# Attention as numerators times a value-output product Y, from seven products of quarters, in an order written by hand

## The chip, the cores and the metric

The kernel runs on one core of a Trainium2 chip. The metric is device time of one launch in microseconds (us), as the median of several runs. A core has five engines that run side by side, each with its own queue of instructions in a fixed order: TensorE (PE) multiplies matrices into PSUM, VectorE (DVE) and ScalarE (ACT) do elementwise work, GpSimd (POOL) does slower elementwise work and can issue transfers, SyncE (SP) issues transfers. An instruction that waits holds everything behind it on its own engine. All data are f32; every f32 product on PE is two instructions with one weight load (PEld) each, called passes here.

## The reference

One transformer block with adaptive layer norm, four batches of 1024 tokens of width 512. Cut to what matters:

```python
mod = (_silu(c) @ wmod).reshape(4, 6, 1, -1)          # sa, ca, ga, sb, cb, gb
ga = (2 * (ga >= 0) - 1) * jnp.maximum(jnp.abs(ga), 0.25)   # gb alike
h = _layernorm(x) * (1 + ca) + sa
qf, kf = h @ Wq.T, h @ Wk.T                            # rank 64, shared by all 16 heads
attn = softmax(qf @ kf.T)                              # 1024 x 1024, the same for each head
x = x + ga * ((attn @ (h @ Wv.T)) @ Wo.T)
h = _layernorm(x) * (1 + cb) + sb
x = x + gb * ((h @ factors.sum(0)) / sqrt(8) + bias)   # eight factors of 512 x 512
```

The scores carry a factor for each head that is one, so all heads have the same probabilities. Wv and Wo can therefore be multiplied into one 512 x 512 matrix, and the softmax's division can be left until the end: the kernels keep numerators (exponents) and scale by the inverse of their sum where the result is added onto x.

## The kernel before

Tokens lie in eight tiles of 128 rows for each batch, x in 16 buffers (two batches). The weights' product `wvo` is made once (line 152). For each batch:

- LN1 (`ln1`): statistics on DVE, the inverse square root as a power on POOL (`rstd_of`, line 276), normalized tokens `xn_a` by DVE (line 290). They are turned into channels-first form `hT_a`: for batch 0 by PE, for the others by a DVE transpose of 32 x 32 blocks and 16 small transfers for each half (`hT_by_dma`, `move_blocks`, line 340), the first half issued by SP, the second by ACT.
- Projection to queries and keys (`project`, line 385), with the scale 1 + ca put into the weights and the shift sa as a bias.
- Scores, exponents, transposition (`scores`, lines 428 to 449; `transpose_probs`, line 455) in four pairs of row tiles: PE, a maximum on DVE, exponents on ACT, a block transpose on DVE, and 16 transfers on SP for each pair.
- Z, the numerators times the normalized tokens, channels first (`z_steps`, line 492, two halves of 512 tokens), copied by ACT; then `attn_out` (line 533): Z times `w` (wvo scaled by 1 + ca and ga), divided and added onto x by DVE (line 538). The constant part that comes from sa is added with `add_c1` (line 332).
- LN2 (`ln2`), its transposition with 16 transfers on ACT for each half (line 569; for the last batch by PE), the scale and shift on ACT (line 572), and the bias added onto x by DVE (line 577).
- `ffn` (line 592): the hidden tile times `f`, the sum of the eight factors scaled by gb; added onto x by DVE (line 597), stored, and x of the batch after next loaded into the buffer.

The sum of the factors (`sum_factors`, lines 259 to 265) is made once, on POOL: 32 loads of 128 x 512 into three buffers, and 28 adds, while batch 0 is in its first Z products. The eight products of F of one batch stand among the Z products of the next. The order in which instructions of each engine stand was set by a scheduler that ranks the steps of the loop at line 630.

Of the kernel before, what the change touches and what calls it, by code (L numbers as in the profile page):

```python
# [10 lines left out]
F32 = mybir.dt.float32  # L11
# [5 lines left out]
def weave(main, fill):  # L17

    done = 0
    for k, step in enumerate(main):  # L20
        step()
        want = (k + 1) * len(fill) // len(main)
        while done < want:
            fill[done]()
            done += 1
    for step in fill[done:]:
        step()
# [3 lines left out]
def kernel(  # L31
# [23 lines left out]
    NT = T // P  # L55
    GT = NT // 2
    GW = GT * P
    Q = 32
# [6 lines left out]
    xnp = ctx.enter_context(tc.tile_pool(name="xnp", bufs=1))  # L65
    stg = ctx.enter_context(tc.tile_pool(name="stg", bufs=3))
    hp = ctx.enter_context(tc.tile_pool(name="hp", bufs=2))
    qkp = ctx.enter_context(tc.tile_pool(name="qkp", bufs=1))
    prp = ctx.enter_context(tc.tile_pool(name="prp", bufs=2))
    stp = ctx.enter_context(tc.tile_pool(name="stp", bufs=1))  # L70
    ptp = ctx.enter_context(tc.tile_pool(name="ptp", bufs=2))
    ztp = ctx.enter_context(tc.tile_pool(name="ztp", bufs=2))
    wbp = ctx.enter_context(tc.tile_pool(name="wbp", bufs=1))
    bcp = ctx.enter_context(tc.tile_pool(name="bcp", bufs=1))
    small = ctx.enter_context(tc.tile_pool(name="small", bufs=4))
    dram = ctx.enter_context(tc.tile_pool(name="dram", bufs=1, space=bass.MemoryType.DRAM))
    ps_s = ctx.enter_context(tc.tile_pool(name="ps_s", bufs=2, space=PSUM))
    ps_m = ctx.enter_context(tc.tile_pool(name="ps_m", bufs=4, space=PSUM))

    def psum_mm(name):  # L80
        return ps_m.tile([P, 512], F32, tag="mm", name=name)


    ident = const.tile([P, P], F32, name="ident")
    make_identity(nc, ident)
    mhalf = const.tile([P, NT], F32, name="mhalf")
    nc.vector.memset(mhalf, -0.5)

# [6 lines left out]
    def load_x(b, t):  # L95
        tl = xp.tile([P, D], F32, tag="x", name=f"x_{b}_{t}")
        nc.sync.dma_start(out=tl, in_=x[b, ts(t, P), :])
        xt[b, t] = tl

    def xn_tile(name):
        return xnp.tile([P, GT, D], F32, tag="xn", bufs=4, name=name)

    wvs, wos = xn_tile("wvs"), xn_tile("wos")
    for cc in range(KC):
        nc.sync.dma_start(out=wvs[:, cc, :], in_=wv[ts(cc, P), :])
        nc.sync.dma_start(out=wos[:, cc, :], in_=woT[ts(cc, P), :])
        for t in range(2 * cc, 2 * cc + 2):
            load_x(0, t)  # L110


    wm_a = ptp.tile([P, 2, KC, D], F32, tag="pt", name="wm_a")
    wm_b = ptp.tile([P, 2, KC, D], F32, tag="pt", name="wm_b")
    wm_c = ztp.tile([P, KC, D], F32, tag="zt", name="wm_c")
    wm_d = ztp.tile([P, KC, D], F32, tag="zt", name="wm_d")
    wmods = [wm_a[:, 0], wm_a[:, 1], wm_b[:, 0], wm_b[:, 1], wm_c, wm_d]

    def load_wmod(m):
        nc.sync.dma_start(  # L120
            out=wmods[m], in_=wmod[:, ts(m, D)].rearrange("(kc p) e -> p kc e", p=P)
        )

    load_wmod(0)
    load_wmod(1)
    wqk = const.tile([P, KC, 2 * R], F32, name="wqk")
    nc.sync.dma_start(out=wqk, in_=wqkT.rearrange("(kc p) r -> p kc r", p=P))
    for m in range(2, 6):
        load_wmod(m)

    rows_a = wbp.tile([B, 4, D], F32, tag="w_b", name="rows_a")
    rows_b = wbp.tile([B, 4, D], F32, tag="f_b", name="rows_b")
    biasb = rows_a[:, 3, :]
    nc.sync.dma_start(out=biasb, in_=bias.to_broadcast([B, D]))
    for t in range(NT):
        load_x(1, t)

# [8 lines left out]

    wvo = const.tile([P, KC, D], F32, name="wvo")
    pw = [ps_s.tile([P, T], F32, tag="sc", name=f"ps_wvo_{h}") for h in range(2)]
# [10 lines left out]


    def mod_products(ms, name):
        ps = psum_mm(f"ps_mod_{name}")
        for kc in range(KC):
            for g, m in enumerate(ms):
                nc.tensor.matmul(
                    ps[32 * g : 32 * g + B, :], scT[:, kc, :], wmods[m][:, kc, :],
                    start=(kc == 0), stop=(kc == KC - 1),
                )
        return ps

    def mod_rows(ps, count, dst):
        rows = []
        for g in range(count):
            nc.vector.tensor_copy(dst[:, g, :], ps[32 * g : 32 * g + B, :])
            rows.append(dst[:, g, :])
        return rows

    def channels(rows, name, plus):

        ps = psum_mm(f"ps_ch_{name}")  # L180
        for kc in range(KC):
            nc.tensor.transpose(ps[:, ts(kc, B)], rows[:, ts(kc, P)], ident[0:B, 0:B])
        m = const.tile([P, KC, B], F32, name=f"mod_{name}")
        nc.vector.tensor_scalar(
            m.rearrange("p k b -> p (k b)"), ps[:, : KC * B], plus, None, ALU.add
        )
        return m

    def gate(g, name):

        sg = bcp.tile([B, D], F32, tag="bc_ga", name=f"gsign_{name}")
        ab = bcp.tile([B, D], F32, tag="bc_c", name=f"gabs_{name}")
# [4 lines left out]


    rows_d = {}

    def publish(rows, name):
        d = dram.tile([B, D], F32, name=f"rows_{name}")
        nc.sync.dma_start(out=d, in_=rows)
        rows_d[name] = d

    def spread(name, b):
        tag = f"bc_{name}" if name in ("ga", "gb") else "bc_c"
# [510 lines left out]
```

## Time and profile before

| | |
|---|---|
| median of three runs | 599.99 us (599.4 to 600.7) |
| span of the profiled execution | 596.5 us; the median is 3.5 us above it |
| PE busy | 565.6 us, 95% of the span |
| DVE, ACT, POOL busy | 311.5, 96.8 and 79.8 us |
| largest groups on PE | Z (L492) 225.3 us, F (L592) 112.2, Z times w (L533) 111.9 |
| scores, projections (L428, L385) | 45.9 and 35.2 us |
| transfers | 65.64 MB, 144703 packets |

The profile is of one execution. A page gives busy time of each engine, the span in 40 slices (a digit is a tenth of the slice), a chain of waits that ended last, and the costliest groups: line, engine, operation, output and inputs by the program's names, shapes, count, busy time, mean length in ns, and the idle time before them with its releaser. Passes on PE overlap, so their mean length is not their spacing; spacing is read from a timeline, as (length of a row less its last pass) divided by the count less one.

### The profile page before, as it was taken

The numbers are of one execution on the slowest core, as the hardware profiler recorded it, in microseconds if no ns is written. First come the engines' busy times: TensorE is split into PE (matmuls) and PEld (weight loads), VectorE is DVE, ScalarE is ACT, GpSimd is POOL, SyncE is SP. The second block draws the span as 40 slices with busy tenths as digits, with TensorE's granted clock in tenths as the row PEclk, the third lists the DMA queues.
The fourth block names the chain that finished last, engine by engine and source line by source line (L and its number), as shares of the span: only waits on it lengthen the run. The fifth ranks groups of instructions, "written<-read, shape, count | busy, mean of one in ns | idle before, by whom it ended". The sixth has DMA issues, their size and how long they took to land.

```text
span 596.5 us, 4491 instructions
## 1 busy us (share of the span) xinstructions
PE 565.6 (95%) x1424; PEld 242.9 (41%) x1424; DVE 311.5 (52%) x514; ACT 96.8 (16%) x161; POOL 79.8 (13%) x90
## 2 busy tenths in 40 slices
PE   6988999999999999799999999899999999999997
PEld 2434443334443344234444443333444434444443
DVE  4559903972695186054697168226398333015641
ACT  1224310241012200123012010022104020000010
POOL 1001017788700001000000001000000000000000
PEclk9998899999999999899999999879999999999999
DMA  8941356869267635204237735303316811000011
GB/s 306 381 177 35 85 114 182 215 167 223 86 109 146 193 105 143 70 4 95 49 58 152 207 113 158 83 1 71 71 23 124 187 59 68 0 0 0 2 70 70
DMA packets 144703, 65.64 MB, mean 110 GB/s; under 512 B 115732, under 2 KB 128532, under 8 KB 144680
## 3 DMA queue, kind: packets, MB, share of 16 engines
q1 hardware_dynamic: 84200, 46.47, 27.9%
q10 hardware_dynamic: 57600, 9.45, 8.8%
q0 software_dynamic: 2880, 9.44, 5.7%
q8 instruction: 11, 0.18, 0.1%
q14 instruction: 12, 0.10, 0.1%
HBM read 29.64 MB, written 8.42 MB: 64 GB/s over the span
## 4 chain that ended last, share of the span: by engine, by line
PE 75%; DVE 9%; DMA 4%; SPq 3%; ACTq 3%; issue 2%; ACT 1%; POOL 1%; POOLq 0%; DVEq 0%
PE ps_z L492 28%; PE ps_o L533 18%; PE ps_f L592 15%; PE ps_sc L428 6%; PE ps_qk L385 3%; ACTq L340 3%; PE ps_wvo L152 3%; SPq L340 2%; DVE st_a L353 2%; DVE x L332 2%; DMA hT_a<-st_a 1%; DVE xn_a L290 1%; DMA out_dram<-x 1%; DVE nm L443 1%; DVE w L515 1%
## 5 line engine op out<-in xcount | busy, mean ns | idle before, releaser
L492 PE MATMUL ps_z<-pt,xn_a 128*128 128x512 f32 x512 | 225.3, 595 | 0.0
L492 PEld LDWEIGHTS ps_z<-pt,xn_a 128*128 128x128 f32 x512 | 96.1, 190 | 126.6 <-issue 125.3
L592 PE MATMUL ps_f<-f,hT_f 128*128 128x512 f32 x256 | 112.2, 594 | 5.6 <-ACT hT_f L572 4.2
L533 PE MATMUL ps_o<-w,zt 128*128 128x512 f32 x256 | 111.9, 593 | 0.0
L592 PEld LDWEIGHTS ps_f<-f,hT_f 128*128 128x128 f32 x256 | 47.9, 190 | 65.6 <-issue 54.6
L533 PEld LDWEIGHTS ps_o<-w,zt 128*128 128x128 f32 x256 | 48.1, 190 | 60.4 <-issue 60.0
L538 DVE SCALAR_TENSOR_TENSOR x<-ps_o,ri,x 128x512 f32<-128x512 f32 x32 | 23.5, 743 | 79.7 <-PE ps_o L533 79.7
L597 DVE TENSOR_TENSOR x<-ps_f,x 128x512 f32<-128x512 f32 x32 | 22.0, 687 | 77.1 <-PE ps_f L592 77.1
L446 ACT ACTIVATE pr<-ps_sc,nm 128x1024 f32<-128x1024 f32 x32 | 35.6, 1114 | 123.0 <-DMA hT_f<-xn_f 58.2
L428 PE MATMUL ps_sc<-kT,qT 64*128 64x512 f32 x128 | 45.9, 691 | 8.6 <-DMA hT_a<-st_a 3.8
L502 ACT COPY zt<-ps_z 128x512 f32<-128x512 f32 x32 | 18.7, 585 | 214.1 <-PE ps_z L492 205.0
L276 POOL TENSOR_TENSOR r_f<-v_f,mhalf 128x4 f32<-128x4 f32 x8 | 9.3, 1158 | 286.6 <-DVE v_f L272 286.6
L443 DVE TENSOR_REDUCE nm<-ps_sc 128x1 f32<-128x1024 f32 x32 | 37.5, 1206 | 7.3 <-PE ps_sc L428 7.2
L385 PE MATMUL ps_qk<-hT_a,wqk 128*128 128x512 f32 x64 | 35.2, 704 | 2.8 <-DMA hT_a<-st_a 1.9
L455 DVE STREAM_TRANSPOSE pr<-pr 128x2048 f32<-128x2048 f32 x14 | 32.2, 2299 | 0.4
L264 POOL TENSOR_TENSOR fsum<-fsum,factor 128x512 f32<-128x512 f32 x24 | 30.9, 1288 | 1.6 <-DMA factor<-in_factors_dram 1.1
L428 PEld LDWEIGHTS ps_sc<-kT,qT 64*128 64x128 f32 x128 | 14.2, 203 | 36.5 <-ACT kT L403 12.6
L399 DVE TENSOR_SCALAR qT<-ps_qk,qbias 64x512 f32<-64x512 f32 x8 | 5.9, 742 | 43.4 <-PE ps_qk L385 43.4
L276 POOL TENSOR_TENSOR r_a<-v_a,mhalf 128x4 f32<-128x4 f32 x8 | 8.5, 1068 | 123.4 <-DVE v_a L272 123.4
L281 DVE BATCH_NORM_STATS2 bn_a<-x 128x6 f32<-128x512 f32 x32 | 21.0, 672 | 7.5 <-DMA x<-in_x_dram 7.4
L332 DVE TENSOR_TENSOR x<-x,bc_c 128x512 f32<-128x512 f32 x32 | 23.7, 792 | 1.4 <-DMA bc_c<-rows_c 1.4
L385 PEld LDWEIGHTS ps_qk<-hT_a,wqk 128*128 128x128 f32 x64 | 14.0, 227 | 24.2 <-issue 20.5
(87 smaller groups left out, 317.9 us busy)
## 6 DMA issues: line engine op xcount, KB each, us to landing
pt<-pr SPq DMA_DIRECT2D x224, 64.0 KB, 2.1
x<-in_x_dram SPq DMA_DIRECT2D x32, 256.0 KB, 4.0
factor<-in_factors_dram POOLq DMA_DIRECT2D x32, 256.0 KB, 3.4
out_dram<-x SPq DMA_DIRECT2D x32, 256.0 KB, 2.3
hT_f<-xn_f ACTq DMA_DIRECT2D x96, 64.0 KB, 2.1
hT_a<-st_a SPq DMA_DIRECT2D x48, 64.0 KB, 2.3
hT_a<-st_a ACTq DMA_DIRECT2D x48, 64.0 KB, 2.1
wm_a<-in_wmod_dram SPq DMA_DIRECT2D x2, 1024.0 KB
```

The source lines that it names most:

```text
L264: nc.gpsimd.tensor_tensor(fsum[:, kc, :], acc, f, ALU.add)
L332: nc.vector.tensor_tensor(xt[b, t], xt[b, t], bc, ALU.add)
L340: queue.dma_start(out=dst[ts(c, Q), :, ts(r, width)], in_=src[ts(r, Q), :, c])
L385: nc.tensor.matmul(ps[: 2 * R, :], wqkb[b][:, kc, :], hT[:, kc, :], start=(kc == 0), stop=(kc == KC - 1),)
L428: nc.tensor.matmul(ps[:, ts(h, 512)], qT[h * R : (h + 1) * R, ts(i, P)], kT[h * R : (h + 1) * R, :], start=True, stop=True,)
L443: nc.vector.tensor_reduce(nm, ps, AX.X, ALU.max, negate=True)
L446: nc.scalar.activation(pr, src, AF.Exp, bias=nm, scale=1.0, accum_out=den[:, k : k + 1])
L455: nc.vector.transpose(pr2, pr2)
L492: nc.tensor.matmul(hold[dc], xn1[b, jh][:, j - jh * GT, ts(dc, P)], PT[b, half][:, j, :], start=(j == 0), stop=(j == NT - 1),)
L533: nc.tensor.matmul(ps, ZT[b, half][:, kc, ts(j, P)], wb[b][:, kc, :], start=(kc == 0), stop=(kc == KC - 1),)
L538: nc.vector.scalar_tensor_tensor(xi, ps, rinv[b][:, t : t + 1], xi, ALU.mult, ALU.add)
L592: nc.tensor.matmul(ps, hT2[b, g][:, kc, ts(j, P)], fb[b][:, kc, :], start=(kc == 0), stop=(kc == KC - 1),)
```

## The change

Instead of Z, the changed kernel makes Y, the hidden tokens times `w` (`y_tile`, now with scale and shift of LN1 applied to the hidden tile itself by `shift_h`), and then adds numerators times Y onto the tokens. This product is made pair by pair of row tiles with seven products of quarters (`o_product`): the numerators of a pair are 2 x 2 quarters of 128 rows by 512 columns, Y is 2 x 2 quarters of 512 rows by 256 columns; `sum_probs` (DVE) and `sum_y` (DVE in batch 0, POOL in the others) make the sums that the scheme of seven needs. The partial results stay in PSUM and grow there; after each product DVE adds what is in the bank onto one half of a token tile, so that a product into the same bank waits for that add. Everything that goes into channels-first form, LN2 of all batches too, goes by a DVE block transpose and 16 transfers on SP (only LN1 of batch 0 is turned by PE). The factors are loaded whole, and added in two halves each. The constant `c1` and the probabilities' transposes on PE go; the bias of F is added by POOL.

There is no scheduler now. A small `Plan` collects calls with a beat (a beat is meant as one pass of 512 columns) and runs them sorted by beat, then by the order of their entry; each engine's queue follows that order.

```diff
+class Plan:
+    def at(self, beat, fn, *args):
+        self.work.append((beat, len(self.work), fn, args))
+    def pe(self, beats, fn, *args):
+        self.at(self.now, fn, *args)
+        self.now += beats
+        return self.now
+    def run(self):
+        for _, _, fn, args in sorted(self.work, key=lambda w: w[:2]):
+            fn(*args)
...
-    stg = ctx.enter_context(tc.tile_pool(name="stg", bufs=3))
+    prp = ctx.enter_context(tc.tile_pool(name="prp", bufs=3))
+    wfp = ctx.enter_context(tc.tile_pool(name="wfp", bufs=2))
...
-                f = stg.tile([P, D], F32, tag="stg", name=f"factor_{kc}_{r}")
-                nc.gpsimd.dma_start(out=f, in_=factors[r, ts(kc, P), :])
-                if r > 0:
-                    nc.gpsimd.tensor_tensor(fsum[:, kc, :], acc, f, ALU.add)
+    def load_factor(r):
+        fac[r] = wide(wfp, "wf", f"factor_{r}")
+        nc.gpsimd.dma_start(
+            out=fac[r], in_=factors[r].rearrange("(kc p) e -> p kc e", p=P)
+        )
+    def add_factor(r, half):
+        k = ts(half, KC // 2)
+        nc.gpsimd.tensor_tensor(
+            fsum[:, k, :], fac[0][:, k, :] if r == 1 else fsum[:, k, :], fac[r][:, k, :], ALU.add
+        )
+    def scale_w(b, kc, eng):
+        if kc == 0:
+            wb[b] = wide(wfp, "wf", f"w_{b}")
+        eng.tensor_tensor(wb[b][:, kc, :], wvo[:, kc, :], bcs["ga", b], ALU.mult)
...
+    def rstd(ln, b, g):
+        v = small.tile([P, GT], F32, tag="rs_v", name=f"v{ln}_{b}_{g}")
+        nc.vector.tensor_scalar(v, mv[ln, b][:, ts(g, GT), 1], EPS, None, ALU.add)
+        rs[ln, b, g] = small.tile([P, GT], F32, tag="rs_r", name=f"r{ln}_{b}_{g}")
+        nc.gpsimd.tensor_tensor(rs[ln, b, g], v, mhalf, ALU.pow)
...
+    def sum_probs(b, p):
+        nc.vector.tensor_tensor(s[:, 0], a21, a22, ALU.add)
+        nc.vector.tensor_tensor(s[:, 1], s[:, 0], a11, ALU.subtract)
+        nc.vector.tensor_tensor(a21, a11, a21, ALU.subtract)
+        nc.vector.tensor_tensor(s[:, 2], a12, s[:, 1], ALU.subtract)
+    def y_tile(b, t):
+        for kc in range(KC):
+            nc.tensor.matmul(
+                ps, h_rows(1, b, t, kc), wb[b][:, kc, :], start=(kc == 0), stop=(kc == KC - 1)
+            )
+        nc.scalar.copy(Y[b][:, t, :], ps)
...
+    def o_product(b, p, n):
+        tag = {1: "y", 5: "q", 2: "x"}.get(n)
...
+        ps = ps_o["y", p] if n in (1, 6, 7, 4) else ps_o["q" if n in (5, 3) else "x"]
+        a, bb = o_operands(b, p, n)
+        for j in range(GT):
+            nc.tensor.matmul(
+                ps, a[:, ts(j, P)], bb[:, j, :], start=(tag is not None and j == 0), stop=(j == GT - 1),
+                skip_group_check=tag is None,
+            )
+        def add(k, e):
+            t = 2 * p + k
+            xi = xt[b, t][:, ts(e, H)]
+            nc.vector.scalar_tensor_tensor(
+                xi, ps, rinv[b][:, t : t + 1], xi, ALU.mult, ALU.add
+            )
+        add(*{1: (0, 0), 5: (1, 1), 6: (0, 1), 2: (0, 0), 7: (1, 1), 3: (0, 1), 4: (1, 0)}[n])
...
+    def plan_ln1(b, at0):
+        for g in range(2):
+            s = at0 + 44 * g
+            for j in range(GT):
+                at(s + 5 * j, stats, 1, b, g * GT + j)
+            at(s + 5 * GT, rstd, 1, b, g)
+            for j in range(GT):
+                at(s + 5 * GT + 5 + 2 * j, normalize, 1, b, g, j)
+            at(s + 34, turn_h, 1, b, g)
+            at(s + 35, move_h, 1, b, g)
+            for kc in range(KC):
+                at(s + 66, shift_h, 1, b, g, kc, nc.scalar)
+    def plan_ln2(b, g, ready):
...
+        at(ready + 14, turn_h, 2, b, g)
+        at(ready + 15, move_h, 2, b, g)
...
+    def plan_o(b):
+        s = plan.now
+        if b + 1 < B:
+            plan_ln1(b + 1, s)
+            at(s, spread, "ga", b + 1)
+            for kc in range(KC):
+                at(s + 60, scale_w, b + 1, kc, nc.vector if b == 0 else nc.gpsimd)
+        at(s, spread, "gbias", b)
+        if b == 0:
+            for r in range(NR):
+                at(s + 1, load_factor, r)
+                if r:
+                    for half in range(2):
+                        at(s + 1, add_factor, r, half)
+        at(s - (40 if b else 16), sum_probs, b, 0)
+        at(s - (34 if b else 0), sum_probs, b, 1)
+        for p in range(NP):
+            if 0 < p < NP - 1:
+                at(plan.now + 3, sum_probs, b, p + 1)
+            for n in (1, 4, 5, 6, 2, 7, 3):
+                if n != 4:
+                    pe(4, o_product, b, p, n)
+                elif p:
+                    pe(4, o_product, b, p - 1, 4)
...
+                        plan_ln2(b, p // 2 - 1, plan.now + 2)
+        pe(4, o_product, b, NP - 1, 4)
+        plan_ln2(b, 1, plan.now + 1)
...
+    plan_start()
+    plan_scores_and_y(0)
+    for b in range(B):
+        last = b + 1 == B
+        if b > 0:
+            plan_f(b - 1, range(GT if last else NT))
+        plan_o(b)
+        plan_scale_f(b, plan.now + (30 if not last else -60))
+        if not last:
+            for g in range(2):
+                pe(8, project, b + 1, g)
+                at(plan.now, qk_out, b + 1, g)
+            plan_scores_and_y(b + 1)
+        else:
+            plan_f(b - 1, range(GT, NT))
+            plan_f(b, range(NT))
+    with tc.manual_schedule():
+        plan.run()
```

`y_tile` and the scores of one row tile alternate (`plan_scores_and_y`: 8 and 2.25 beats, eight times); F of one tile is 8 beats, followed by the store of the tile and the load of x of the batch after next, both on SP.

## The prediction

> **What bounds the kernel now.** I read the engine shares first, then the slices, the costliest groups, and last the timelines of PE, POOL and SP, where spacings can be read. The page says that TensorE is the bound nearly everywhere:
>
> ```profile
> PE 565.6 (95%) x1424; PEld 242.9 (41%) x1424; DVE 311.5 (52%) x514; ACT 96.8 (16%) x161; POOL 79.8 (13%) x90
> ...
> PE   6988999999999999799999999899999999999997
> ...
> L492 PE MATMUL ps_z<-pt,xn_a 128*128 128x512 f32 x512 | 225.3, 595 | 0.0
> L492 PEld LDWEIGHTS ps_z<-pt,xn_a 128*128 128x128 f32 x512 | 96.1, 190 | 126.6 <-issue 125.3
> ...
> L264 POOL TENSOR_TENSOR fsum<-fsum,factor 128x512 f32<-128x512 f32 x24 | 30.9, 1288 | 1.6 <-DMA factor<-in_factors_dram 1.1
> ...
> L276 POOL TENSOR_TENSOR r_a<-v_a,mhalf 128x4 f32<-128x4 f32 x8 | 8.5, 1068 | 123.4 <-DVE v_a L272 123.4
> ```
>
> PE has no idle digit; DVE is half used; POOL has time to spare and its sums wait for nobody. The timeline of PE (start, length, group) gives the true price of a pass (each f32 product is two instructions, called passes here):
>
> ```profile
> 30.14 1.05 PE L223 MATMUL ps_qbias<-mod_sa,wqk 128*128 128x4 f32 x8
> ...
> 251.13 5.57 PE L385 MATMUL ps_qk<-hT_a,wqk 128*128 128x512 f32 x8
> ...
> 307.91 13.90 PE L492 MATMUL ps_z<-pt,xn_a 128*128 128x512 f32 x32
> ```
>
> 32 passes in 13.90, the last lasting 0.60: one each 0.429 us. Weight loads (0.19 us) hide completely. The first row is passes of four columns, so it shows weight loads alone: (1.05-0.25)/7 = 0.114 us each. The middle row is eight passes after a 3.83 us gap: 5.57 instead of 3.6, the granted clock being 0.77 in that stretch.
>
> The timeline of POOL shows the factor sum, which I need below: issue, wait, add, in order.
>
> ```profile
> 106.03 0.57 POOL L262 DMA_DIRECT2D factor<-in_factors_dram  x1 [0.30 <-POOL fsum L264]
> 108.28 1.53 POOL L264 TENSOR_TENSOR fsum<-factor,factor 128x512 f32<-128x512 f32 x1 [1.69 <-DMA factor<-in_factors_dram]
> 110.11 1.11 POOL L262 DMA_DIRECT2D factor<-in_factors_dram  x2 [0.30 <-POOL fsum L264]
> ```
>
> And SP's timeline with the table of transfers (last column: us to landing) shows what a block move and a large load cost:
>
> ```profile
> 65.00 21.36 SPq L340 DMA_DIRECT2D pt<-pr  x32
> ```
>
> ```profile
> factor<-in_factors_dram POOLq DMA_DIRECT2D x32, 256.0 KB, 3.4
> ...
> wm_b<-in_wmod_dram SPq DMA_DIRECT2D x2, 1024.0 KB, 12.6
> ```
>
> 32 moves in 21.36: 0.667 each, so the 16 moves of one pair of score rows, or of one half of a hidden tile, hold SP for 10.7 us, and land 2.1 later.
>
> **The change, part by part.**
>
> *PE work.* Before: 512 + 256 passes for Z and its product. After: 256 passes of 512 for Y, and per batch 4 x 7 products of 4 x 2 passes of 256 columns: 896 in all. A 256-column pass was never run. Below: half of 0.429, 0.215; above: the weight load no longer hides fully, 0.19 + 0.05 = 0.24 (the spacing in which it would end before the next starts). I take 0.215, because loads alone follow each other every 0.114. So 1120+8 passes of 512 become 1058 equivalents (32 V-O product, 64 projections, 256 Y, 256 F, 448 quarters, 2 gate row); 32 probability and 32 hidden transposes go. PE work after: 1058 x 0.429 = 454, plus scores 32 x 0.96 = 31 (eight passes of L428 in 1.92), two modulation products 7, transposes and small ones 5: 497. With the first load (5.3, the idle before L152) and the tail after the last product (596.5 - 592.4 = 4.1): 506 if nothing waited. That is the promise of the change.
>
> [...]
>
> *Factor sum on POOL, batch 0.* This decides. The eight factors are now loaded whole (1 MB) into two buffers shared with w, and summed as two adds of 1024 elements each. In the built order POOL has load 0, load 1, add 1, load 2, add 2, load 3 ...; each load sits behind the adds of the one before, so nothing overlaps, and the first load that counts (factor 1) takes the buffer of w and waits for the last Y product. Per factor: issue 0.57 + landing + two adds 2 x 2.5 (1.28 per 512) + 0.3 (the wait behind POOL's own sum). Landing of 1 MB: below 2.2 (what 256 KB needed at 106.03), above 12.6 (wm_b, in a crowd). 256 KB took 3.4; three more quarters at the 381 GB/s of the second 15 us are 2.1: 5.5, nearest to the factor row. So 11.4 per factor, 7 of them 80 us. [...]
>
> Behind these adds on POOL stands rstd of the next batch's first half (1.1 us). Behind that rstd, on DVE, the normalize of that half; and behind the normalize all further adds of the quarter products, which read PSUM before PE may accumulate on. So when does PE run dry? Start to Y: 40 us (before: first projection at 31.65; then gate row, scaling of w four times 0.69, second projection), 5 more than PE's own work. Y and scores of batch 0: 39.5, quarters begin at 79. PE does pair 0 and five products of pair 1, with sums of Y (4 x 1.2 on DVE) in its way: dry at 79 + 23 = 102. POOL: 78 + 80 + 1.1 = 159. DVE then first does what is queued ahead of the awaited add: four normalizes 1.9, sums of a pair 2.7, a transpose 2.3, stats 1.7, adds: 9.5. PE goes on at 169. Lost: 67, plus 4 before and 6 after, when DVE has 29 us of work beside 29 us of products: 77.
>
> *From O to the next projection.* All 16-move groups now queue on SP; ACT issued hT_f and half of hT_a before. In plan order: first hidden half of the next batch, then LN2's first half, then the second hidden half. LN2's transpose is planned 33 us into the quarters, so the second half lands 33 + 2 x 10.7 + 2.1 = 56, first shift 0.8: 57, where PE arrives after 48.2 + 3.4 = 51.6 (or later by what the quarters lose). With DVE's own lag at the transposes 7.5 us wait, then eight passes at the lower clock (2.5, as at 251.13), then 2 for q and k, whose copies on ACT stand behind eight shifts: 12, three times: 36.
>
> *DVE in the quarters of batches 1 and 2.* 28 adds, half as wide as L538 (743): between 0.37 and 0.74, I take 0.45; LN1 of the next batch 14, two pairs of sums 5.4, LN2 11, adds 13: 44 of 48 us, in fixed order. A 2.3 us transpose or a 2.7 us sum before an add that PE needs within one product (1.72) costs 1.5 to 4 each time: 7. x of batch b+2 comes late: SP ends the probability moves 18 us after Y, then alternates out and load (0.6 + 2.3 + 0.6, eight times), so the fourth tile lands some 2 us after DVE asks. 9 twice, 2 in the last batch: 20.
>
> *Costed at nothing:* c1 and bias adds (DVE, 24 + 20 us) go or move to POOL, beside PE both times; block sums of Y on POOL (10 us) lie beside 27 us of F; LN2's last half (8 + 10.7 + 2.1 + 3.3 = 24) lies under 27.4 of F products. If that cover failed, the tail would grow by the difference.
>
> *Sum* against the profiled execution (596.5): 506 + 5 + 77 + 36 + 20 = 644. The median of the runs shown, 599.99, is 3.5 above it: 647. I say 645.
>
> **The rivals.**
>
> - *Shorter chain:* the 1 MB load lands in 2.2 us as if it were 256 KB. For: these loads have the queues to themselves. 8.1 x 7 = 57: 23 less, 622.
> - *Weight loads show:* 0.24 per pass. For: 0.19 of 0.215 leaves 0.025. 896 x 0.025 = 22: 667.
> - *Longer chain:* landing 12.6, 7 x 7 = 50 more: 695. Against: that row was taken beside seven other megabytes.
> - *Faster after all:* the factor sum hides. Its place is POOL between the last Y product and rstd; the change gains if the chain costs 47 us less, under 33 us, 4.7 per factor. For: POOL's queue might be free by then, PE has 23 us of cover. Against: the two adds alone are 5.0 by L264, unless a wide add costs much less than two narrow ones. If it hid completely: 645 - 67 = 578.
>
> **How the numbers follow.** The forecast 0.62 (own range 628 to 662: landing 4 to 7.5, waits of DVE and SP a third up or down), shorter chain 0.14, weight loads 0.12, longer 0.06, faster 0.05, no change 0.01. The range 613 to 682 takes in the forecast and the two next cases with their own spread. About 0.2% is what a measurement of this kernel tells from no change. Slower 0.94, same 0.01, faster 0.05.
>
> **What would show it.** One gap of some 65 us in PE's digits, from about 102 us, DVE idle in it with "xn/st <- POOL r", POOL with 14 adds near 2.5 us and waits for factor of about 5 between; quarter products every 0.215 us; PE busy near 520; three gaps of 7 us before the second projections, released by ACT's shift behind SP moves; DVE late on PSUM in quarters of batches 1 and 2. I am wrong if PE has no long gap in batch 0, or if 256-column passes are spaced like 0.3 and more.

## The result, and the profile after

The changed kernel takes 665.81 us (median of four runs, 662.64 to 666.46) against 600.35 for the kernel before on the same chip (four runs, 599.4 to 601.1). The ratio is 1.109, with a 95% interval of 1.105 to 1.112: slower by 65 us. The forecast was 645, between 613 and 682. The profiled execution has a span of 664.6 us, 68 more than before.

The page of the changed kernel (busy time; the 40 slices; costliest groups with count, busy us, mean ns, idle before and who ended it; the factor transfers with KB and us to landing):

```profile
PE 541.0 (81%) x1730; PEld 311.7 (47%) x1730; DVE 357.2 (54%) x546; ACT 115.1 (17%) x184; POOL 160.3 (24%) x112
...
PE   6899926600678599998875899997985999899997
...
L486 PE MATMUL ps_o_y<-y,pt 128*128 128x256 f32 x256 | 68.3, 414 | 62.0 <-DVE x L494 62.0
...
L280 DVE TENSOR_SCALAR st<-x,mv,r 128x512 f32<-128x512 f32 x56 | 42.3, 799 | 49.4 <-POOL r L274 46.9
...
L241 POOL TENSOR_TENSOR fsum<-fsum,factor 128x1024 f32<-128x1024 f32 x12 | 29.6, 2484 | 31.6 <-DMA factor<-in_factors_dram 31.6
...
factor<-in_factors_dram POOLq DMA_DIRECT2D x8, 1024.0 KB, 6.0
```

PE has fewer products to do and is busy for less time, but it now has a hole: the sixth digit is 2 and the ninth and tenth are 0 (a slice is 16.6 us), where before none but the first was under 7. The groups give the chain of causes backwards: PE's quarter products waited 62.0 us for DVE's adds onto x, DVE's normalizations waited 46.9 us for r from POOL, and POOL's adds of factors waited 31.6 us for the factors' transfers.

The timeline of PE shows the hole in place (start, length, group; in brackets the idle time before and who ended it):

```profile
85.18 1.99 PE L486 MATMUL ps_o_y<-y,pt 128*128 128x256 f32 x8
102.04 3.75 PE L486 MATMUL ps_o_q<-yt,s 128*128 128x256 f32 x8 [14.87 <-DVE yt L459]
...
120.60 1.89 PE L486 MATMUL ps_o_y<-yt,pt 128*128 128x256 f32 x8
122.33 1.89 PE L486 MATMUL ps_o_q<-yt,s 128*128 128x256 f32 x8
...
125.78 1.89 PE L486 MATMUL ps_o_x<-y,pt 128*128 128x256 f32 x8
171.84 3.56 PE L486 MATMUL ps_o_y<-y,pt 128*128 128x256 f32 x8 [44.17 <-DVE x L494]
```

Two things are to be read here. From 120.60 to 125.78 nothing is in the way: three products of eight passes take 5.18 us, 1.727 each, which is 0.216 us a pass. The products do cost what they were meant to cost. And there is one gap of 44.17 us, after a first one of 14.87. The timeline of POOL over the same time, and what DVE was waiting for:

```profile
125.49 4.64 POOL L241 TENSOR_TENSOR fsum<-fsum,factor 128x1024 f32<-128x1024 f32 x2 [5.56 <-DMA factor<-in_factors_dram]
130.07 0.77 POOL L235 DMA_DIRECT2D factor<-in_factors_dram  x1
135.68 4.63 POOL L241 TENSOR_TENSOR fsum<-fsum,factor 128x1024 f32<-128x1024 f32 x2 [4.84 <-DMA factor<-in_factors_dram]
...
161.32 1.03 POOL L274 TENSOR_TENSOR r<-v,mhalf 128x4 f32<-128x4 f32 x1
```

```profile
162.38 1.00 DVE L280 TENSOR_SCALAR st<-x,mv,r 128x512 f32<-128x512 f32 x2 [41.10 <-POOL r L274]
```

Each factor takes about 11 us: issue, wait for the landing, add, and only then the next issue. The chain runs from 84.50 (load of factor 1) to 161.3, 77 us, and the one rstd (the inverse square root of LN1, line 274) that stands behind it releases DVE, which releases PE 9.5 us later.

### The profile page after: what moved, and what is told of

It is laid out like the page before. It is cut to its first block, busy times and chain, and to the rows that moved or that the text cites. A ratio compares the mean times of both kernels' runs of the same rounds, so it can differ in the third digit from the quotient of the medians.

```text
span 664.6 us, 5417 instructions
## 1 busy us (share of the span) xinstructions
PE 541.0 (81%) x1730; PEld 311.7 (47%) x1730; DVE 357.2 (54%) x546; ACT 115.1 (17%) x184; POOL 160.3 (24%) x112
## 4 chain that ended last, share of the span: by engine, by line
PE 42%; DVE 17%; SPq 16%; DMA 14%; POOL 6%; issue 3%; ACT 1%; DVEq 0%; ACTq 0%; POOLq 0%
SPq L300 16%; PE ps_y L444 11%; PE ps_f L505 8%; DMA factor<-in_factors_dram 6%; PE ps_o_y L486 6%; POOL fsum L241 5%; PE ps_qk L365 4%; DVE st L280 4%; PE ps_o_q L486 3%; DMA out_dram<-x 3%; PE ps_sc L392 3%; PE ps_wvo L160 3%; DVE st L304 2%; DMA hT<-st 2%; DVE bn L267 2%
## 5 line engine op out<-in xcount | busy, mean ns | idle before, releaser
L486 PE MATMUL ps_o_y<-y,pt 128*128 128x256 f32 x256 | 68.3, 414 | 62.0 <-DVE x L494 62.0
L444 PE MATMUL ps_y<-w,hT 128*128 128x512 f32 x256 | 118.0, 604 | 0.0
L505 PE MATMUL ps_f<-f,hT 128*128 128x512 f32 x256 | 111.1, 594 | 0.2 <-ACT hT L319 0.2
L319 ACT ACTIVATE hT<-hT,chan,chan 128x512 f32<-128x512 f32 x60 | 43.6, 805 | 382.3 <-DMA hT<-st 381.5
L486 PEld LDWEIGHTS ps_o_y<-y,pt 128*128 128x128 f32 x256 | 52.4, 208 | 74.6 <-DVE x L494 64.8
L444 PEld LDWEIGHTS ps_y<-w,hT 128*128 128x128 f32 x256 | 46.3, 189 | 68.5 <-issue 68.5
L505 PEld LDWEIGHTS ps_f<-f,hT 128*128 128x128 f32 x256 | 48.3, 190 | 62.2 <-issue 58.9
L280 DVE TENSOR_SCALAR st<-x,mv,r 128x512 f32<-128x512 f32 x56 | 42.3, 799 | 49.4 <-POOL r L274 46.9
L267 DVE BATCH_NORM_STATS2 bn<-x 128x6 f32<-128x512 f32 x64 | 43.3, 677 | 13.4 <-DMA x<-in_x_dram 13.2
L509 DVE TENSOR_TENSOR x<-ps_f,x 128x512 f32<-128x512 f32 x32 | 21.7, 685 | 51.6 <-PE ps_f L505 51.6
L515 POOL TENSOR_TENSOR x<-x,bc_gbias 128x512 f32<-128x512 f32 x32 | 44.2, 1396 | 9.7 <-DVE st L280 9.7
L494 DVE SCALAR_TENSOR_TENSOR x<-ps_o_y,ri,x 128x256 f32<-128x256 f32 x64 | 29.9, 473 | 27.6 <-PE ps_o_y L486 27.3
L241 POOL TENSOR_TENSOR fsum<-fsum,factor 128x1024 f32<-128x1024 f32 x12 | 29.6, 2484 | 31.6 <-DMA factor<-in_factors_dram 31.6
```

What stands on the lines that cost most here:

```text
L241: nc.gpsimd.tensor_tensor(fsum[:, k, :], fac[0][:, k, :] if r == 1 else fsum[:, k, :], fac[r][:, k, :], ALU.add)
L267: nc.vector.bn_stats(s, xt[b, t])
L280: nc.vector.tensor_scalar(st[ln, b, g][:, :, :, j].rearrange("p c k e -> p k c e"), xt[b, t].rearrange("p (k c e) -> p k c e", k=KC, c=NQ) ...
L319: eng.activation(v, v, AF.Identity, bias=shift, scale=scale)
L444: nc.tensor.matmul(ps, h_rows(1, b, t, kc), wb[b][:, kc, :], start=(kc == 0), stop=(kc == KC - 1))
L486: nc.tensor.matmul(ps, a[:, ts(j, P)], bb[:, j, :], start=(tag is not None and j == 0), stop=(j == GT - 1), skip_group_check=tag is None,)
```

## Experiments

All comparisons are with runs of the kernel before on the same chip. A span is that of the run's profiled execution; spans are set against spans (664.6 for the changed kernel), ratios against the kernel before.

### The chain of factors: how much of it, and where

**Two factors only.**

```diff
-            for r in range(NR):
+            for r in range(2):
                 at(s + 1, load_factor, r)
```

> Leaves factors 2 to 7 out of the sum (their loads and adds), so F is computed with two factors of eight. Theory (the chain of loads and adds on POOL holds the rstd of batch 1, this holds DVE's normalize, this holds the adds that PE waits for): POOL's chain shrinks from 77 us to about 12, the 44 us gap of PE at 128 us goes, the wait for the Y sums at 87 us stays; quarters of batch 0 take about 80 us instead of 126, the median falls by some 46 to 620. Rival (the quarters of batch 0 lose because DVE has too much to do there): the same 126 us within 15, the median above 650.

Measured: 616.65 us, ratio 1.029 (1.018 to 1.040), span 615.3. Two of PE's waits in the quarters of batch 0 of this kernel:

```profile
98.22 3.75 PE L486 MATMUL ps_o_q<-yt,s 128*128 128x256 f32 x8 [13.08 <-DVE yt L459]
...
138.92 3.78 PE L486 MATMUL ps_o_y<-y,pt 128*128 128x256 f32 x8 [3.56 <-DVE x L494]
```

The long gap is gone, and with it 49 us of span. The gap of 44 us hangs on six rounds of load and add. The 13 us wait for the sums of Y stays: it has another cause.

**Each load one step ahead of the adds.**

```diff
                 at(s + 1, load_factor, r)
-                if r:
+                if r > 2 or r == 1:
                     for half in range(2):
-                        at(s + 1, add_factor, r, half)
+                        at(s + 1, add_factor, max(r - 1, 1), half)
+            for half in range(2):
+                at(s + 1, add_factor, NR - 1, half)
```

> The same POOL instructions, each load issued one step earlier, before the add of the factor before it. Theory: load (5.5) and add (4.65) now lie beside each other, about 5.8 us per factor for the last five or six instead of 11.0; the chain takes 52 us instead of 77, the gap ends 25 us earlier, the median is 641. Rival (loads and POOL's adds slow each other, or the gap is not the chain's): above 655.

Measured: 643.18 us, ratio 1.073 (1.061 to 1.085), span 640.1. The gap in PE's timeline is now:

```profile
144.60 3.78 PE L486 MATMUL ps_o_y<-y,pt 128*128 128x256 f32 x8 [26.91 <-DVE x L494]
```

Half of each round was waiting for a transfer that could have been under way. Hiding it gives 24.5 us; the adds alone still leave 27 us of gap.

**The order by hand taken away.**

```diff
-    with tc.manual_schedule():
-        plan.run()
+    plan.run()
```

> The changed kernel with the order by hand taken away: the same operations, put in order by the framework's scheduler with its own priorities. Theory (the time is lost in the order in which POOL and SP are handed the sum of the factors and the moves of h): a scheduler that lets the rstds past the factor adds should lose some of the 44 us gap, so below 664.6; I put it at 645, between 620 (all of the long gap gone) and 665 (same order kept). Rival (the loss is in the products themselves, which any order must pay): 660 to 670 with the gaps spread differently. Above 675 would say that the order by hand is worth its place and that only its sum of the factors is badly placed.

Measured: 693.9 us, ratio 1.156 (1.144 to 1.168), span 693.3. I had expected 645 and was wrong. PE's timeline has

```profile
144.59 4.63 PE L486 MATMUL ps_o_y<-yt,s 128*128 128x256 f32 x10 [34.24 <-DVE yt L459]
```

and DVE's has the reason, a row that stands between the first and the second of the sums of Y:

```profile
140.56 0.69 DVE L250 TENSOR_TENSOR w<-wvo,bc_ga 128x512 f32<-128x512 f32 x1 [33.36 <-POOL fsum L241]
```

The scheduler let the rstd past the factors, but put the scaling of w for batch 1 between the sums of Y on DVE; w takes a buffer that a factor holds until it is added, so the same chain of factors again stops DVE, by another door. Batches 1 and 2 lose too, their quarters taking 75 us instead of 62, and the last batch's take 66 instead of 50.5. So the order by hand is better than this scheduler's, and its costliest fault is the place of one instruction in POOL's queue (49 us of span, by the kernel with two factors).

### The first wait, for the sums of Y

DVE's sums of Y waited 9.63 us for a transfer: the tile that they write is the one from which the rows of gb are published, and that publish stood on SP behind 48 moves of the pairs. Does this wait cost time of its own, or does it lie inside the longer one?

```diff
-        nc.sync.dma_start(out=rows_d[name], in_=src)
+        (nc.sync if name == "ga" else nc.gpsimd).dma_start(out=rows_d[name], in_=src)
```

> The rows gb and gbias are published by a transfer that POOL issues, not SP, where they stood behind the moves of the third pair; so DVE's sums of Y no longer wait for them (9.6 us) nor PE for those sums (14.9 us). Theory: no gain, 664 to 667, because DVE and PE only come earlier to the wait for POOL's chain, whose end is unchanged; PE's long gap grows by what the first wait loses. Rival (waits add up): 15 us less, 651.

Measured: 673.41 us, ratio 1.124 (1.112 to 1.135), span 671.8.

```profile
175.80 3.78 PE L486 MATMUL ps_o_y<-y,pt 128*128 128x256 f32 x8 [66.82 <-DVE x L494]
```

The first wait shrank from 14.87 to 5.14 us and the second grew from 44.17 to 66.82: the waits don't add, because POOL's chain alone sets when PE goes on. It even went on later (175.80 instead of 171.84), since the two publishes stood on POOL ahead of factor 0, which until then had been loaded long before; now it came with factor 1, and the chain ended at 165.3. Of the 7.2 us of span, 4.0 are this later start; by the first Y product of batch 1 the kernel is 6.0 us behind (234.25 instead of 228.27): 1.1 more came in the quarters that were left and 0.9 around the second projection.

### From the quarters to the next projections

**Moves of the next batch's h issued by ACT.**

```diff
-            st[ln, b, g].rearrange("p c k t e -> p (c k t e)"), h_tile(ln, b, g), apart=ln == 2
+            st[ln, b, g].rearrange("p c k t e -> p (c k t e)"), h_tile(ln, b, g), apart=ln == 2,
+            queue=nc.scalar if ln == 1 else nc.sync,
```

> The 16 moves of each half of the first hidden tile of batches 1 to 3 are issued by ACT, the rest stays on SP. Theory (second projection waits because LN2's moves stand before its half on SP): the three waits of 8.4, 8.8 and 7.3 us go, and with them the slow passes after them (1.6, 2.9, 2.7); 30 us less, 636. Rival (ACT is held by the issues, 0.65 each, so that its shifts and the copies of q and k come late instead): less than 10 us gained, 656 or more.

Measured: 638.99 us, ratio 1.066 (1.055 to 1.077), span 637.4. The second projection of batch 1, first in the changed kernel and then in this one:

```profile
223.28 5.16 PE L365 MATMUL ps_qk<-hT,wqk 128*128 128x512 f32 x8 [8.35 <-DMA hT<-st]
```

```profile
213.90 3.70 PE L366 MATMUL ps_qk<-hT,wqk 128*128 128x512 f32 x8 [0.51 <-ACT hT L320]
```

The wait goes from 8.35 to 0.51 us, and the eight passes after it from 5.16 to 3.70: the granted clock in them is 0.70 in the changed kernel and 1.00 here. Three such places give the 27 us.

**Both edits together** (loads one step ahead, ACT's moves).

> The two single edits together: each factor load issued one step earlier, and the moves of h for the next batch issued by ACT. Theory (the two losses stand in different places, the first inside O of batch 0, the second between O and the next projections): they add, 664.6 - 23 - 27 = 615 span. Rival (they share a cause, the wait for h of batch 1, so one covers part of the other): 625 to 635.

Measured: 614.56 us, ratio 1.024 (1.017 to 1.031), span 612.0. They add, to within 1 us of span (664.6 - 24.5 - 27.2 = 612.9): two separate losses.

### Can the sum of the factors be hidden?

**Adds spread over the quarters.** The sum is kept whole; every rstd stands ahead of the adds that it doesn't need. ACT's moves as above.

```diff
-            for r in range(NR):
-                at(s + 1, load_factor, r)
-                if r:
-                    for half in range(2):
-                        at(s + 1, add_factor, r, half)
+            for beat, adds, loads in (
+                (1, (), (0, 1)), (1, (1,), (2, 3)), (21, (2,), (4,)), (34, (3,), (5,)),
+                (68, (4,), (6,)), (82, (5,), (7,)), (96, (6,), ()), (97, (7,), ()),
+            ):
+                for r in adds:
+                    for half in range(2):
+                        at(s + beat, add_factor, r, half)
+                for r in loads:
+                    at(s + beat, load_factor, r)
...
-                at(s + 60, scale_w, b + 1, kc, nc.vector if b == 0 else nc.gpsimd)
+                at(s + (60 if b else 118), scale_w, b + 1, kc, nc.vector if b == 0 else nc.gpsimd)
```

> The moves of h issued by ACT, and all seven factors summed as before but with POOL's adds spread over O of batch 0 (beats 1, 21, 34, 68, 82, 96, 97 of its 112), so that each rstd stands ahead of the adds that it doesn't need; w of batch 1 is scaled at beat 118, since its buffer comes free late. Theory (POOL's 80 us is harmless by itself; what costs is that the rstd of batch 1 stands behind it): the 44 us gap goes as it did with two factors, 616 - 27 = about 590, faster than the kernel before by some 10 us. Rival 1 (adds and DVE's normalization slow each other enough to matter): 600 to 605. Rival 2 (w of batch 1, now late, stops Y of batch 1): one new wait of 5 to 15 us on wb before the first y_tile of batch 1, 597 to 605.

Measured: 605.71 us, ratio 1.010 (1.005 to 1.014), span 606.2. The theory's 590 was missed by 16 us; the first rival's 600 to 605 is near. The second rival's wait on w does not show: PE goes from the second projection into Y of batch 1 without one. The quarters of batch 0 take 97 us, 19 more than with two factors. DVE's timeline in them:

```profile
117.38 3.19 DVE L280 TENSOR_SCALAR st<-x,mv,r 128x512 f32<-128x512 f32 x2
120.49 5.66 DVE L431 TENSOR_TENSOR s<-pt 128x512 f32<-128x512 f32 x1
126.17 0.69 DVE L432 TENSOR_TENSOR s<-s,pt 128x512 f32<-128x512 f32 x1
...
151.90 8.67 DVE L280 TENSOR_SCALAR st<-x,mv,r 128x512 f32<-128x512 f32 x4
```

and POOL's:

```profile
115.18 4.64 POOL L241 TENSOR_TENSOR fsum<-fsum,factor 128x1024 f32<-128x1024 f32 x2
...
120.94 4.65 POOL L241 TENSOR_TENSOR fsum<-fsum,factor 128x1024 f32<-128x1024 f32 x2
...
151.84 4.83 POOL L241 TENSOR_TENSOR fsum<-fsum,factor 128x1024 f32<-128x1024 f32 x2
```

A sum of a pair that takes 0.69 us took 5.66, and ended 0.6 us after POOL's two adds that began 0.45 us into it. Two normalizations took 3.19 instead of 1.00, four took 8.67 instead of 2. That is 13.8 us of DVE in these rows, of which 1.8 stand in the changed kernel too (its four normalizations at 191.03 took 3.80, beside POOL's adds of the bias). The 12.0 that are new and the 7.1 by which the first wait is longer (20.21 us here, 13.08 with two factors) make up the 19 us. POOL's adds stay near their 4.6 us (4.64 to 4.83). So in these rows it is DVE that takes longer: its sum is shown 0.45 us ahead of the two adds and yet ends after both, if the starts shown for POOL are exact. Why it does, the rows don't tell.

**Rows of gb by POOL, factor 0 loaded ahead of them**, otherwise as the kernel just told.

```diff
-        nc.sync.dma_start(out=rows_d[name], in_=src)
+        (nc.sync if name == "ga" else nc.gpsimd).dma_start(out=rows_d[name], in_=src)
...
     def plan_scores_and_y(b):
+        if b == 0:
+            at(plan.now, load_factor, 0)
...
-                (1, (), (0, 1)), (1, (1,), (2, 3)), (21, (2,), (4,)), (34, (3,), (5,)),
+                (1, (), (1,)), (1, (1,), (2, 3)), (21, (2,), (4,)), (34, (3,), (5,)),
```

> The kernel with the spread sum and ACT's moves, and also the rows of gb and its bias published by POOL instead of SP, with factor 0 loaded ahead of them. Theory (DVE's sums of Y waited 9.6 us for the rows' publish, which stood on SP behind the moves of the pairs, and PE's first quarters waited for them): the wait of 14 us on yt in batch 0 shrinks to about 5, and with the long gap gone nothing takes its place: 590 - 10 = about 580. Rival (the time comes back at the next wait of O of batch 0, on x or on h): 588 to 592.

Measured: 601.76 us, ratio 1.003 (0.999 to 1.007), span 602.6. The wait for the sums of Y fell from 20.21 to 5.14 us and the quarters of batch 0 from 97 to 87 us, so shortening this wait, which gained nothing in the changed kernel, gives 10 us of the quarters where POOL's chain no longer decides. (Factor 0 is loaded early here; in the kernel with the publish alone it wasn't.) The forecast of 580 counted from 590, a level that the kernel without the edit had not reached. Of the 10 us, 3.6 show in the span: in this execution the quarters of batch 0 already began 4.2 us later (85.7 instead of 81.5), ahead of the wait in question, and a wait of 2.3 us for h came before the second projections. The median falls by 4.0.

**Factors added by DMAs instead of POOL.** Eight transfers write or add into one tile; the loads of factors no longer need w's buffers.

```diff
-        fac[r] = wide(wfp, "wf", f"factor_{r}")
-        nc.gpsimd.dma_start(
-            out=fac[r], in_=factors[r].rearrange("(kc p) e -> p kc e", p=P)
-        )
+        src = factors[r].rearrange("(kc p) e -> p kc e", p=P)
+        if r == 0:
+            nc.gpsimd.dma_start(out=fsum, in_=src)
+        else:
+            nc.gpsimd.dma_start(out=fsum, in_=src, accum_op=ALU.add)
...
     def plan_scores_and_y(b):
+        if b == 0:
+            for r in range(3):
+                at(plan.now + 30 * r, load_factor, r)
...
+            for r, beat in ((3, 1), (4, 26), (5, 45), (6, 70), (7, 90)):
+                at(s + beat, load_factor, r)
```

> As the kernel with ACT's moves and the rows of gb published by POOL, but POOL adds no factors: eight DMAs write factor 0 and add factors 1 to 7 to the sum in place, at beats spread over Y and O of batch 0. Theory (what kept the spread sum above 600 is that a DVE instruction that meets one of POOL's adds stands until the add ends, 5.66 instead of 0.69 us for one sum of a pair, 8.67 instead of 2.0 for four normalizations; some 15 us of DVE in O of batch 0): with the adds gone from POOL O of batch 0 takes 70 to 75 us instead of 87 and the span is 602.6 - 14 = about 588, faster than the kernel before by 10 us or more. Rival (O of batch 0 is held by DVE's own work or by h of batch 1, whatever POOL does): 598 to 604. A third way: a DMA that adds is slower than one that writes (6 us) and holds up POOL's rstds; then a wait on r by DVE of 5 us or more would show, and 600 or above.

Measured: 597.27 us, ratio 0.996 (0.993 to 0.999), span 596.6. The sums of pairs are back at 0.69 us each, so it was POOL's adds that had stretched them; but the quarters of batch 0 take 81 us, not 70 to 75, and the 10 us or more that the theory promised against the kernel before became 2.5. What holds the quarters is mostly new: PE waits 14.00 us at 139.25 for DVE (3.68 at the same product in the changed kernel, at 189.44), and DVE waits 10.63 us for the last pair. DVE first, then SP and ACT's queue:

```profile
130.31 0.69 DVE L432 TENSOR_TENSOR s<-pt 128x512 f32<-128x512 f32 x1 [10.63 <-DMA pt<-pr]
```

```profile
97.29 30.87 SPq L301 DMA_DIRECT2D pt<-pr  x16
```

```profile
110.92 16.23 ACTq L301 DMA_DIRECT2D hT<-st  x16
```

The sixteen moves of one pair spread over 30.87 us; in the changed kernel they took 12.44 (from 113.33), with two factors 10.68. SP's list of waits in this stretch has six on ACT's moves of h, 19.0 us in all. The two groups share no data, and h is normalized later: it is a false wait, one that no value needs. Why moves on one queue stood behind moves on the other, the traces don't tell. The same sixteen moves lasted 69.5 us in the first kernel with ACT's moves, where they were hidden by the long gap, and 29.0 in the one with the spread sum.

**Scores of two tiles together**, in the changed kernel.

```diff
-            p, k = divmod(t, 2)
-            if p >= 0:
+            p, last = divmod(t, 2)
+            for k in range(2 * last):
                 pe(2.25, scores, b, p, k)
```

> The changed kernel with one edit: in the sections of Y, the scores of two tokens' tiles follow one another after every second tile of Y, instead of one after each tile, so PE changes between the two kinds of product 16 times fewer in all. Theory (each change between Y's 128-row passes and the scores' 64-row passes costs about 0.3 us, which made these sections 37.4 us instead of 35.2): 16 x 0.3 = 4.8 us less, span 660, the sections at about 36.2. Rival 1 (the passes themselves are longer there, not the change between them): 664 to 665, sections at 37.4. Rival 2 (the softmax of the last pair ends later and DVE's sums of the pair with it): sections at 36.2, but O waits longer at its start, 665 to 669.

Measured: 666.0 us, ratio 1.110 (1.102 to 1.118), span 662.9. PE's timeline of Y, first in the changed kernel, then in this one:

```profile
232.86 3.70 PE L444 MATMUL ps_y<-w,hT 128*128 128x512 f32 x8
236.49 1.13 PE L392 MATMUL ps_sc<-kT,qT 64*128 64x512 f32 x4
237.55 3.70 PE L444 MATMUL ps_y<-w,hT 128*128 128x512 f32 x8
```

```profile
233.37 1.99 PE L392 MATMUL ps_sc<-kT,qT 64*128 64x512 f32 x8
235.29 7.13 PE L444 MATMUL ps_y<-w,hT 128*128 128x512 f32 x16
242.35 1.99 PE L392 MATMUL ps_sc<-kT,qT 64*128 64x512 f32 x8
```

A tile with its scores takes 237.55 - 232.86 = 4.69 us, and (242.35 - 233.37) / 2 = 4.49 when two go together. Rows without such changes would give 3.43 + 0.96 = 4.39, so half as many changes take away 0.20 of the 0.30 us: the price is in the change from one kind to the other, not in the passes. The granted clock is 1.00 in the sections of batch 1 of both kernels, so it isn't the clock. The kernel before has the price too, where Z stands between scores:

```profile
126.99 3.70 PE L492 MATMUL ps_z<-pt,xn_a 128*128 128x512 f32 x8
130.62 1.99 PE L428 MATMUL ps_sc<-kT,qT 64*128 64x512 f32 x8
```

Eight passes of Z take 130.62 - 126.99 = 3.63 us there instead of 3.43. Eight of a projection between passes of Z, all on 128 rows, take 3.43 (from 99.58 to 103.01): it is the change to 64 rows and back that costs the 0.2 us in these rows, not any change.

The sections shrink to 36 us as expected, but the gain didn't reach the end. Batch 0's lies ahead of the end of POOL's chain. In batches 1 and 2 the sections are 1.6 us shorter and the quarters behind them 1.7 and 1.4 us longer: they begin earlier, and DVE waits for x of the batch after next (6.8 us in each, against 5.1 and 4.3 in the changed kernel). So the time came back at another wait, as the second rival had it, though not at the one that it named. Two runs tell no difference in the time.

**Factors by DMAs and scores in twos.**

> The kernel whose factors are summed by DMAs, with the scores of two tiles together in the sections of Y as well. If both theories hold, 588 - 5 = about 583; if the change between products costs nothing, or the later softmax gives it back, 588.

Measured: 594.40 us, ratio 0.9925 (0.989 to 0.996), span 591.8: 4.8 less in the span, 2.9 in the median of twelve runs each. The 583 counted from 588, which the kernel without the edit had missed; the difference of 5 is what the span shows. The four sections gave 7.2 us together, and the quarters took 3.1 more.

**The first half of h back on SP.** Only the second half is moved by ACT. The false wait named below is that of the last pair of batch 0, whose moves on SP wait for ACT's moves of h.

```diff
-            queue=nc.scalar if ln == 1 else nc.sync,
+            queue=nc.scalar if ln == 1 and g == 1 else nc.sync,
```

> The fastest kernel so far (factors summed by DMAs, scores in twos, rows of gb by POOL) with one edit: of the two hidden halves of the next batch only the second is moved by ACT, the first by SP again. [...] Theory (this false wait kept DVE 10.6 us and PE 14.8 us in O of batch 0): with the first half back on SP the sixteen moves take 12 us, the wait of 14.8 us goes, O of batch 0 takes 67 to 70 us instead of 82, span 591.8 - 13 = about 579. Rival 1 (the pair's moves are slow because the DMA engines are busy with the factors): they stay at 30 us and the span at 590 to 593. Rival 2 (SP is too long a queue again for the first half): a new wait of 5 us or more for h before the second batch's projections, 585 to 590.

Measured: 587.20 us, ratio 0.977 (0.973 to 0.982), span 584.2: faster than both kernels; 14 us less than the one before on the same chip (601.51). SP's timeline, and PE's wait for the last pair (14.80 without the edit):

```profile
95.78 18.51 SPq L301 DMA_DIRECT2D pt<-pr  x16
```

```profile
130.52 3.78 PE L488 MATMUL ps_o_y<-y,pt 128*128 128x256 f32 x8 [7.54 <-DVE x L496]
```

SP no longer waits for h within these moves. DVE's wait for the pair falls from 11.43 to 4.17 us and PE's with it: the false wait is shown. The quarters of batch 0 take 75 us, not 67 to 70. Of the 7.54 us that PE still waits, 3.6 were never part of the false wait: PE waits 3.56 us at the same product with two factors, where the pair is there in time and only DVE's own queue is in the way. The other 4 are the pair: its moves take 18.5 us, not 12. Single issues last up to 2.25 us (0.63 usual), and the last two land after some 9 us (2.3 usual), while two factors are being added by DMA. That speaks for the first rival as the rest of the story, but no run separated it, so it stays open. The second rival's wait for h before the second projections is there, 4.27 us, but it isn't new: it was 4.15 without the edit.

## Why the prediction was right, point by point

The sign, the place and the cause were right, and the sum was 20.6 us short of the span (644 against 664.6).

- *PE work.* 0.215 us a pass taken, 0.216 measured: weight loads of 0.19 to 0.21 us stay hidden beside 256 columns. The rival that they show is refuted by the spacing itself; that the total came out near its 667 is chance. **The step that failed** is "scores 32 x 0.96" and Y tiles at 8 x 0.429: the prices were read where passes of one kind follow one another. In the changed kernel a tile and its scores take 4.69 instead of 3.43 + 0.96 = 4.39, 0.3 x 32 = 9.6 us that are in no term. The run with scores in twos shows that alternating causes most of it, and the profile before showed the price already, in the eight passes of 3.63 us at 126.99. PE was busy 541 us where 520 was put: these 9.6 us, and 10 more in the quarters of batch 0, where PE was busy 58.5 us for 48.2 us of products, at a mean granted clock of 0.72.
- *Start.* Y was put at 40 and began at 43.6; in other runs with the same start it began between 40 and 44, so the 3.6 us belong to this execution: 3.0 of them are the first projection, whose eight passes took 6.72 us at a granted clock of 0.54 (3.70 at 1.00 in the kernel with loads one step ahead).
- *Factor sum.* 80 us forecast, 77 measured; 11.4 a factor against 11.0 (the two adds 4.64 where 5.0 was taken); PE resumes at 171.8, forecast 169; lost 78, forecast 77. The 1 MB landed in 6.0 us where 5.5 was taken. With two factors the loss went. But I had PE dry at 102 and it was dry at 127.7: the 15 us wait for the sums of Y, behind the publish on SP, wasn't seen. So the 78 us are divided otherwise: 23.5 before the gap, 44 in it and 10 after it, where 4, 67 and 6 were put. The sum agrees because the chain's end was right, not because its parts were. The wait itself cost nothing, since the end of the chain sets when PE goes on; the run with the publish on POOL shows that it gains nothing to shorten it there.
- *From O to the next projection.* 36 forecast (three times 12), measured 10.1 + 11.9 + 10.2 = 32. Cause and size confirmed by ACT's moves, 27 us.
- *DVE in the quarters.* 20 forecast; the quarters took 61.6 us in batches 1 and 2 and 50.5 in the last, against 48.2 of products: 13.4 + 13.4 + 2.3 = 29. The add was 0.47, taken 0.45, so the missing 9 us lie elsewhere: in batch 1, PE's waits for DVE make 10.0 of the 13.4, and 3.4 are passes that last longer (51.6 us busy). The wait of some 2 us that was foreseen for one tile of x came for three (0.8, 2.1 and 2.2 us on DVE). Part of DVE's lag is time that the sum didn't have: beside POOL's adds of the bias, four normalizations took 3.81 and 3.80 us (at 334.56 and 479.05) instead of 2.0 and the next three 2.22 instead of 1.5, some 2.5 us of DVE in each batch. No run shows how much of it reaches PE.
- *Costed at nothing:* F stayed at 27.6 us, so its covers held.
- *The rivals.* Shorter and longer chain: the landing decided against both. "Faster after all" needed the chain under 33 us or hidden, 578 if it hid completely. It did become true, but in another kernel: with the factors summed by DMAs, the moves divided between two queues, the publish on POOL and the scores in twos, the products of quarters take 587.

The balance: 506 of PE's work and ends + 9.6 of alternation + 8.6 to Y + 78 + 32 + 29 = 663 of 664.6.

## What to carry to other kernels

A saving in products is collected only if everything that was hidden under the longer ones still is: list what each in-order queue holds ahead of the one small instruction that the next stage waits for (here a 1 us rstd behind 77 us of loads and adds). Of several waits in one stretch, only the one that ends last costs time: shortening the wait for the publish gained nothing while POOL's chain decided, and gave 10 us of the quarters once it didn't. A price per instruction that is read where one kind follows itself leaves out what the change to another kind costs: read it where the two alternate (here 4.69 us instead of 4.39 for a tile and its scores). When work goes to a free engine or a second queue, read what the first one's instructions take beside it: here a sum of a pair on DVE took 5.66 us instead of 0.69 beside POOL's adds, and a pair's moves on SP 30.87 us instead of 12.44 once ACT moved h.

## What the hardware showed that I had not expected

- Beside POOL's adds of factors DVE's instructions took longer: 5.66 instead of 0.69 us for a sum of a pair, 8.67 instead of 2.0 for four normalizations; with the factors added by DMAs the sums took 0.69 again. In the changed kernel both engines took longer: two sums of Y 3.37 us each instead of 1.23, the pair of POOL's adds beside them 6.43 instead of 4.64.
- Moves on SP waited for moves on ACT with which they share no data (six waits, 19.0 us in all): sixteen moves that took 12.4 us took 29 to 70, and 18.5 with the first half of h back on SP.
- A transfer that adds 1 MB in place landed in 9.5 us (median of eight, the plain first one among them), one that writes it in 6.0; its issue held POOL 1.3 us instead of 0.77. It kept POOL and DVE free, and was worth it here: 6.0 us of span (602.6 to 596.6), though it met the false wait.
- Changing between products of 64 and of 128 rows on PE and back cost 0.2 us where eight passes of scores stand together and 0.3 where four do, at a granted clock of 1.00.
